# The last stage of an eight-layer kernel: a routing table summed on TensorE and tokens gathered by it, blocks of two sizes, and half of the shared expert moved behind them

## The chip, the cores and the metric

The kernel runs on one core of a Trainium2 chip. The metric is the time of one execution on the device, in microseconds (us), as the median of the runs shown. Everything computed is float32.

## The reference, cut to what matters

Eight layers follow one another on a residual `x` of 8 x 512 tokens of 256 numbers. Each adds `layernorm(layer(layernorm(x)))`. The first seven are not touched. The last one is a mixture of eight experts with a shared expert:

```python
xf = x.reshape(-1, 256)                       # 4096 tokens
scores = softmax(xf @ w_router)               # 8 experts
expert_weights, expert_indices = top_k(scores, 2)
cw = zeros((4096, 8)).at[arange(4096)[:, None], expert_indices].add(expert_weights)
h = silu(einsum('td,edh->teh', xf, w1)) * einsum('td,edh->teh', xf, w3)   # 512 wide
moe_out = einsum('te,ted->td', cw, einsum('teh,ehd->ted', h, w2))
shared = silu(xf @ ws1) * (xf @ ws3) @ ws2
out = shared / 3 + moe_out * (2 / 3)
```

Each token needs only its two experts, so there are 2 x 4096 = 8192 rows of expert work. Which rows go to which expert is known on the chip only.

## The kernel before

The kernel is written in a tile language: pools hand out buffers, a scheduler lays the instructions of each engine in one fixed order, and semaphores join the engines. SP issues most of the transfers, POOL the indirect ones. A buffer is written again only when its last reader is done, and an instruction that waits holds up all that stands behind it on its engine. The seventh layer (`l3_attn`, lines up to 1690) ends at about 4619 us of the profiled span. All that follows is `l3_ffn`.

**Routing.** `route(b)` runs for each of 8 batches of 512 tokens. It normalizes (L1788), transposes on TensorE (L146), copies to `xT` on ScalarE (L148), multiplies by the router (L1796, `pl`), takes Exp on ScalarE (L1803) and the two best experts on VectorE (L1810, L1811), and leaves one-hot tables `O[0]`, `O[1]` (L1820). The normalized rows stay in SBUF in `xnr`, 260 numbers wide: 256 of data, the token's number, two of its weights and its first expert. `places()` then sums the one-hots (L1829, L1834) and derives on VectorE the position of each token's row among rows sorted by expert (L1843 to L1873), where each expert's rows are filled up to a multiple of `BK` = 256, and the expert `ei` of each block (L1886).

**Sorting through DRAM.** 64 indirect transfers (L1963), one for each 128 tokens and each of their two experts, write the rows of `xnr` to their places in `xs`. `xs` was first filled with a neutral row by one transfer of 10 MB on ScalarE's queue (L1730), and each of the 64 waits for that.

**The shared expert.** `shared(b)` runs for all 8 batches before the blocks. `experts` multiplies by two matrices of 256 x 512 (L1755, `gs`), applies Silu on ScalarE (L1760) and the product on VectorE (L1761). `down` multiplies by the third matrix (L1769). The result, times 1/3 (L1894), is stored to `acc` in DRAM (L1896) and loaded again as `yl` (L1979).

**The blocks.** There are 39 blocks of 256 rows: `NBLK = (8192 + 8 * 255) // 256`, whatever the routing is. `block(j)` reads its expert's number into a register of SP (L1906), loads the three weight matrices of 512 KB each (L1740) into a pool with two buffers for each, and loads 256 rows of `xs` (L1912). Nine small instructions on POOL (L1918 to L1931) compute the weight and the destination of each row. TensorE transposes (L1935, `pxb`), VectorE copies (L1938, `xbT`), `experts` and `down` follow with 256 rows as the moving operand, ScalarE applies the weight (L1943), and two indirect transfers on POOL (L1944) write the rows to `ys`, two rows for each token.

**The end.** For each batch two loads of `ys` (L1992) wait for every one of the indirect writes, and VectorE adds them to `yl` (L1997). `add_norm` follows: statistics on VectorE, here with Ln and Exp on ScalarE (L111, L112) for the inverse root because `K.log_exp` is set, the scaling on ScalarE (L172), the addition to `x` on POOL (L174), and the store of the output (L2019).

PSUM is cut into two banks for `pmm` (transposes and routing), four for `pG` (the first two products) and two for `pY` (the third).

Of the kernel before, what the change touches and what calls it, by code (L numbers as in the profile page):

```python
# [1692 lines left out]
def l3_ffn(K):  # L1693
# [4 lines left out]

    nc, tc = K.nc, K.tc
# [5 lines left out]
    BK = 256  # L1705
    NBLK = (2 * NB * L + E * (BK - 1)) // BK
    with ExitStack() as es:
        def pool(name, bufs, **kw):
            return es.enter_context(tc.tile_pool(name="f3" + name, bufs=bufs, **kw))
        dr = pool("dr", 1, space=DRAM)  # L1710

        R_ID, R_DW, R_W1, R_E0, R_END = D, D + 1, D + 2, D + 3, D + 4
        xs = dr.tile([NBLK * BK, R_END], F32, name="xs")
        acc = dr.tile([NB * L, D], F32, name="acc")
        ys = dr.tile([2 * NB * L + 1 + NBLK * BK, D], F32, name="ys")
        cst, wp, sb, s1, s3 = pool("c", 1), pool("w", 2), pool("a", 2), pool("b", 1), pool("d", 3)
        sx = pool("x", 5)
# [4 lines left out]
        zero = cst.tile([P, R_END], F32, name="zero")  # L1722
        nc.vector.memset(zero, 0.0)
        zi = cst.tile([P, 1], I32, name="zi")
        nc.gpsimd.iota(zi, [[1, 1]], base=2 * NB * L + 1, channel_multiplier=1)
        nc.vector.tensor_copy(zero[:, R_ID:R_ID + 1], zi)
        half = cst.tile([P, 2], F32, name="half")
        nc.vector.memset(half, 0.0)
        nc.vector.memset(half[:, 1:2], float(P))
        cleared = nc.scalar.dma_start(  # L1730
            out=xs.rearrange("(n p) d -> p n d", p=P),
            in_=zero[:, None, :].to_broadcast([P, NBLK * BK // P, R_END]))
        ti = cst.tile([P, TT], I32, name="ti")
        nc.gpsimd.iota(ti, [[2 * P, TT]], base=1, channel_multiplier=2)

        def load_weights(src, uid, sel):
            ts = []
            for nm, s, k in zip(("w1", "w3", "w2"), src, (2, 2, 4)):
                t = wp.tile([P, k, s.shape[-1]], F32, tag=nm, name=f"{nm}_{uid}")
                nc.sync.dma_start(out=t, in_=sel(s).rearrange("(k p) n -> p k n", p=P))  # L1740
                ts.append(t)
            return ts

        def experts(xT, n, ws, uid):
# [3 lines left out]
            hT = (s1 if n == L else sb).tile([P, 4, n], F32, tag=f"hT{n}", name=f"hT{uid}")  # L1748
# [15 lines left out]
        def down(hT, ts, w2, uid):  # L1764

            ps = pY.tile([P, 2, D], F32, tag="y", name=f"y{uid}")
            for j, n in enumerate(ts):
                for c in range(4):
                    nc.tensor.matmul(  # L1769
                        ps[:, j, :], lhsT=hT[:, c, n * P:(n + 1) * P], rhs=w2[:, c, :],  # L1770
                        start=(c == 0), stop=(c == 3))
            return ps

        def shared_weights(uid):
            return load_weights([i["l3f_s1"], i["l3f_s3"], i["l3f_s2"]], uid, lambda s: s)


        XN, O = [], []
        for j in range(2):
            O.append(cst.tile([P, E, TT], F32, name=f"O{j}"))  # L1780

        def route(b):
            xn = cst.tile([P, NT, R_END], F32, name=f"xnr{b}")
            XN.append(xn)
            x = K.X[b]
            mv, r = K.stats([x[:, n, :] for n in range(NT)], "ln")
            for n in range(NT):
                nc.vector.tensor_scalar(  # L1788
                    xn[:, n, 0:D], x[:, n, :], mv[:, n, 0:1], r[:, n:n + 1], ALU.subtract, ALU.mult)

            dst = spare[:, b - 5] if b >= 5 else None
            t = K.norm_T(b, sx, pmm, "mm", xn=xn, dst=dst)
# [21 lines left out]
            nc.vector.tensor_scalar(v8, v8, 2.0 / 3.0, None, ALU.mult)  # L1814
            nc.gpsimd.tensor_copy(xn[:, :, R_ID], ti[:, b * NT:(b + 1) * NT])
            nc.vector.tensor_tensor(xn[:, :, R_DW], v8[:, :, 0], v8[:, :, 1], ALU.subtract)
            nc.gpsimd.tensor_copy(xn[:, :, R_W1], v8[:, :, 1])
            nc.gpsimd.tensor_copy(xn[:, :, R_E0], f8[:, :, 0])
            for j in range(2):
                nc.vector.tensor_tensor(  # L1820
# [3 lines left out]
            return t  # L1824

        def places():

            M = cst.tile([P, E, TT], F32, name="M")
            nc.vector.tensor_tensor(M, O[0], O[1], ALU.add)  # L1829
            ones = cst.tile([P, P], F32, name="ones")  # L1830
            nc.vector.memset(ones, 1.0)
            ps = pmm.tile([P, 2, E, TT], F32, tag="mm", name="prank")
            for j, t in enumerate((K.up, ones)):
# [4 lines left out]
            keep = cst.tile([P, E, TT], F32, name="keep")  # L1838
            nc.vector.memset(keep, 1.0)
            nc.vector.memset(keep[:, :, 0:1], 0.0)  # L1840
            cnt = cst.tile([P, E, TT], F32, name="cnt")
# [5 lines left out]
            nb = cst.tile([P, E], F32, name="nb")  # L1847
            nbi = cst.tile([P, E], I32, name="nbi")
            nc.vector.tensor_scalar(nb, cnt[:, :, TT - 1], BK - 1.0, None, ALU.add)
            nc.vector.tensor_copy(nbi, nb)  # L1850
            nc.vector.tensor_single_scalar(
                nbi, nbi, BK.bit_length() - 1, ALU.arith_shift_right)
            nc.vector.tensor_copy(nb, nbi)
            end = cst.tile([P, E], F32, name="end")
            nc.vector.tensor_tensor_scan(end, ones[:, 0:E], nb, 0.0, ALU.mult, ALU.add)
            base = cst.tile([P, E], F32, name="base")
            nc.vector.tensor_tensor(base, end, nb, ALU.subtract)

            pos = cst.tile([P, E, TT], F32, name="pos")
# [3 lines left out]
            nc.vector.scalar_tensor_tensor(  # L1863
                pos, base[:, :, None].to_broadcast([P, E, TT]), float(BK), pos,
                ALU.mult, ALU.add)
            rows = []
            for j in range(2):
                t = cst.tile([P, E, TT], F32, name=f"pj{j}")
                nc.vector.tensor_tensor(t, O[j], pos, ALU.mult)
                f = cst.tile([P, TT], F32, name=f"pf{j}")  # L1870
                nc.vector.tensor_reduce(f, t.rearrange("p e n -> p n e"), AX.X, ALU.add)
                r = cst.tile([P, TT], U32, name=f"row{j}")
                nc.vector.tensor_copy(r, f)  # L1873
                rows.append(r)
            jt = cst.tile([P, NBLK], I32, name="jt")
            nc.gpsimd.iota(jt, [[1, NBLK]], base=0, channel_multiplier=0)
            jf = cst.tile([P, NBLK], F32, name="jf")
            nc.gpsimd.tensor_copy(jf, jt)
            ge = cst.tile([P, NBLK, E - 1], F32, name="ge")
            nc.vector.tensor_tensor(  # L1880
                ge, jf[:, :, None].to_broadcast([P, NBLK, E - 1]),
                end[:, None, 0:E - 1].to_broadcast([P, NBLK, E - 1]), ALU.is_ge)
            ef = cst.tile([P, NBLK], F32, name="ef")
            nc.vector.tensor_reduce(ef, ge, AX.X, ALU.add)
            ei = cst.tile([1, NBLK], I32, name="ei")
            nc.vector.tensor_copy(ei, ef[0:1, :])  # L1886
            return rows, ef, ei
# [95 lines left out]
        for j in range(NBLK):  # L1983
            block(j)
# [115 lines left out]
```

## Time and profile before

| What | us |
|---|---|
| median of 3 runs (5361.62 to 5367.62) | 5366.64 |
| profiled execution, its own time | 5409.07 |
| its span | 5407.4 |
| end of the seventh layer | 4619 |
| routing, places, sorting, shared expert | 4619 to 4894 |
| 39 blocks | 4894 to 5337 |
| the end | 5337 to 5407 |

The profile is of one execution. Its engines are PE (TensorE's matmuls), PEld (its weight loads), DVE (VectorE), ACT (ScalarE), POOL (GpSimd) and SP (the queue of transfers). The times of rows are counted from the start of the span. A float32 matmul shows as two instructions, a transpose as one. The chain of waits follows the last instruction back to what released it, step by step; the timeline gives instructions in order of time; a table of stretches gives the busy time of each engine in a stretch, the number of instructions behind it, the granted clock of TensorE, the busy share of the 16 DMA engines and the GB/s that they moved.

### The profile page before, as it was taken

How to read it: one execution, taken by the hardware profiler on the slowest of the kernel's cores; microseconds unless marked ns; L12 is line 12 of the kernel's file. 1: busy time of each engine (PE TensorE's matmuls, PEld its weight loads, DVE VectorE, ACT ScalarE, POOL GpSimd, SP SyncE). 2: the span in 40 equal slices, each digit the busy share in tenths (PEclk: the TensorE clock that was granted, in tenths of full speed). 3: DMA queues.
4: the chain of work that ended last, by engine and by line, in shares of the span. 5: the costliest groups of instructions: out<-in, count | busy, mean ns of one | idle time of the engine just before them, and what ended most of it. 6: DMA issues, size and time to landing. Idle time of an engine off the chain costs nothing.

```text
span 5407.4 us, 56107 instructions
## 1 busy us (share of the span) xinstructions
PE 4455.9 (82%) x18522; PEld 2698.1 (50%) x18522; DVE 3009.1 (56%) x8102; ACT 1895.8 (35%) x3800; POOL 1941.1 (36%) x1571
## 2 busy tenths in 40 slices
PE   8655888999974987888888899788888887679994
PEld 3334765655554974444444455333333333447883
DVE  7999555477684125455555443387777778411114
ACT  5401324343431332333333324355555554211112
POOL 0001213443432441111111100198878889322332
PEclk9777889999997998999999999898999998889997
DMA  4386511000005970000000000011111111425664
GB/s 120 85 202 152 140 33 41 5 9 5 9 23 133 251 195 8 5 5 4 5 5 1 1 20 1 16 53 44 44 44 45 46 43 51 135 76 170 187 186 157
DMA packets 418856, 371.95 MB, mean 69 GB/s; under 512 B 209827, under 2 KB 354933, under 8 KB 418005
## 3 DMA queue, kind: packets, MB, share of 16 engines
q1 hardware_dynamic: 380564, 309.40, 20.8%
q0 software_dynamic: 16320, 31.78, 2.1%
q10 hardware_dynamic: 21680, 27.18, 1.5%
q8 instruction: 147, 2.41, 0.2%
q14 instruction: 145, 1.18, 0.1%
HBM read 282.13 MB, written 85.91 MB: 68 GB/s over the span
## 4 chain that ended last, share of the span: by engine, by line
PE 39%; DVE 15%; POOL 5%; ACT 5%; issue 4%; another core or an unknown queue 1%; DMA 1%; DVEq 0%; POOLq 0%; SPq 0%; ACTq 0%
DVE h L1667 6%; PE gb L1755 5%; PE T L1402 4%; PE h L1234 3%; PE S L1379 3%; PE y L1638 3%; PE g L1495 3%; PE yb L1769 3%; DVE junk L1384 2%; PE py L185 2%; DVE dB L1613 2%; PE pc L1560 2%; PE gs L1755 2%; PE y L1245 2%; POOL h L1670 2%
## 5 line engine op out<-in xcount | busy, mean ns | idle before, releaser
L1670 POOL TENSOR_TENSOR h<-h,C 128x1024 f32<-128x1024 f32 x256 | 595.8, 2355 | 177.2 <-DVE h L1667 139.3
L1638 PE MATMUL y<-h,C 128*128 128x512 f32 x1024 | 533.9, 662 | 103.0 <-POOL h L1670 103.0
L1667 DVE TENSOR_TENSOR_SCAN h<-dA,dB 128x512 f32<-128x512 f32 x512 | 589.3, 1204 | 29.8 <-ACT dA L1664 12.2
L1664 ACT ACTIVATE dA<-dl,A 128x512 f32<-128x512 f32 x512 | 352.6, 691 | 412.2 <-DVE h L1667 411.1
L929 POOL TENSOR_SCALAR p<-p,rs 128x128 f32<-128x128 f32 (+3 forms) x256 | 275.7, 1086 | 384.6 <-DVE rs L928 222.0
L1638 PEld LDWEIGHTS y<-h,C 128*128 128x128 f32 x1024 | 202.1, 208 | 411.9 <-issue 224.6
L1379 PE MATMUL S<-KT,qz 128*128 128x512 f32 (+3 forms) x1024 | 345.3, 473 | 42.8 <-ACT qz L1367 21.3
L174 POOL TENSOR_TENSOR X<-X,yn 128x1024 f32<-128x1024 f32 x64 | 152.6, 2384 | 613.6 <-ACT yn L172 552.6
L1405 ACT ACTIVATE PT<-T 128x256 f32<-128x256 f32 (+3 forms) x512 | 211.6, 437 | 386.6 <-PE T L1402 378.8
L1402 PE MATMUL T<-qz,KT 128*128 128x512 f32 (+3 forms) x1024 | 313.9, 450 | 2.9 <-DVE mx L1384 0.3
L1407 POOL TENSOR_SCALAR_AFFINE_SELECT PT<-PT 128x512 f32<-128x512 f32 x128 | 81.2, 635 | 632.0 <-ACT PT L1405 628.7
L1618 POOL TENSOR_TENSOR dB<-du,B 128x2048 f32<-128x2048 f32 x64 | 289.8, 4528 | 0.1
L1379 PEld LDWEIGHTS S<-KT,qz 128*128 128x128 f32 x1024 | 181.3, 195 | 209.6 <-DVE mx L1384 60.0
L1755 PE MATMUL gb<-xbT,w_b 128*128 128x256 f32 x1248 | 277.2, 380 | 8.3 <-ACT yb L1943 7.9
L1384 DVE CUSTOM_DVE_ANT_0 junk<-S,mask 128x256 f32<-128x256 f32 (+3 forms) x512 | 250.8, 490 | 58.2 <-PE S L1379 12.1
L1755 PEld LDWEIGHTS gb<-xbT,w_b 128*128 128x128 f32 x1248 | 235.5, 190 | 43.7 <-ACT yb L1943 11.9
L1613 DVE TENSOR_TENSOR dB<-du,pb 128x2048 f32<-128x2048 f32 x64 | 145.5, 2275 | 168.3 <-PE pb L1610 118.7
L1402 PEld LDWEIGHTS T<-qz,KT 128*128 128x128 f32 x1024 | 170.8, 192 | 133.9 <-issue 86.1
L1761 DVE TENSOR_TENSOR hTb<-sb,gb 128x512 f32<-128x512 f32 x78 | 53.7, 688 | 297.5 <-PE gb L1755 297.5
L927 ACT ACTIVATE p<-p,nm 128x128 f32<-128x128 f32 (+3 forms) x256 | 143.8, 563 | 197.3 <-DVE nm L923 192.4
L1239 ACT ACTIVATE hT<-h,w_l_ffn 128x128 f32<-128x128 f32 x384 | 109.5, 368 | 219.1 <-PE h L1234 219.1
L1234 PE MATMUL h<-xgT,w 128*128 128x128 f32 x1536 | 183.6, 278 | 0.0
(492 smaller groups left out, 9086.3 us busy)
## 6 DMA issues: line engine op xcount, KB each, us to landing
w_b<-l3f_w SPq DMA_DIRECT2D x117, 512.0 KB
w<-l1f_w SPq DMA_DIRECT2D x48, 1024.0 KB
C<-xdd SPq DMA_DIRECT2D x128, 256.0 KB
B<-xdd SPq DMA_DIRECT2D x64, 256.0 KB
w<-l1f_w SPq DMA_DIRECT2D x48, 256.0 KB
toep<-l0fd SPq DMA_DIRECT2D x32, 320.0 KB
xs<-zero ACTq DMA_DIRECT2D x1, 10140.0 KB
xb<-xs SPq DMA_DIRECT2D x39, 260.0 KB
```

Source lines behind the costliest of these rows:

```text
L929: nc.gpsimd.tensor_scalar(p[:, 0:n], p[:, 0:n], rs, None, ALU.mult)
L1234: nc.tensor.matmul(ph[:, j, :], lhsT=w1[:, s, c, m * P:(m + 1) * P], rhs=xgT[:, c, :], start=(c == 0), stop=(c == 1))
L1379: nc.tensor.matmul(ps[:, 0:n], lhsT=QZ[:, j, qt * P:n], rhs=KT[:, g, 0:n], start=True, stop=True)
L1384: nc.vector.tensor_tensor_reduce(out=junk[:, 0:n], in0=tiles[j][:, 0:n], in1=mask[:, L - n:L], scale=1.0, scalar=-3.0e38, op0=ALU.add, op1 ...
L1402: nc.tensor.matmul(ps[:, 0:n], lhsT=KT[:, g, kt * P:(kt + 1) * P], rhs=QZ[:, j, kt * P:L], start=True, stop=True)
L1613: nc.vector.tensor_tensor(dB, du, pb[:, None, :].to_broadcast([P, 4, L]), ALU.mult)
L1618: nc.gpsimd.tensor_tensor(dB, du, B[:, None, :].to_broadcast([P, 4, L]), ALU.mult)
L1638: nc.tensor.matmul(py[2 * j + c], lhsT=K.ident, rhs=h[:, c, :], start=False, stop=(n == NS - 1))
L1664: nc.scalar.activation(dA, dl[:, c, :], AF.Exp, scale=A[:, c, n:n + 1])
L1667: nc.vector.tensor_tensor_scan(hs[-1][:, c % 2, :], dA, dB[:, c, :], 0.0, ALU.mult, ALU.add)
L1670: nc.gpsimd.tensor_tensor(h, h, C[:, None, :].to_broadcast([P, 2, L]), ALU.mult)
L1755: nc.tensor.matmul(ps[:, q, :], lhsT=ww[:, k, (c + q) * P:(c + q + 1) * P], rhs=xT[:, k, :], start=(k == 0), stop=(k == 1))
```

## The change

Before the blocks:

- `route` keeps the normalized rows in tiles of a two-buffer pool and stores them to `xn_d` in DRAM in token order, one transfer of 512 KB for each batch. The transposed rows stay in `TS[b]`. The fields beside the rows are gone; the two weights are kept in `WT`.
- `places` fills 256-row blocks first: each expert gets as many full blocks of 256 as its count holds, up to 25 (`NBIG`) in all; the rest goes into blocks of 128, of which there are 21 (`NSMALL`). This adds some 20 small VectorE instructions.
- `table` is new. Each row has a place `128 * hi + lo`. For groups of eight columns VectorE builds a matrix `A` with a one at `lo`, a matrix `B` with a one at `hi`, and `V`, which is `B` times the token's number and times its weight. TensorE sums `A^T V` over all 64 columns into one PSUM bank. What comes out is, for each of 71 half blocks of 128 places, the token, its weight, and where its result goes.
- The 10 MB clearing transfer and the 64 indirect writes are gone.
- The shared expert runs for the first four batches here and leaves its result in SBUF, in `TS[b]`; the store to `acc` and the load back are gone.

In the blocks: a block of 256 is followed by one of 128 as long as there are any, four blocks of 256 come last. Each half block's rows are gathered by an indirect transfer on POOL from `xn_d`, into a pool of six buffers. The nine small POOL instructions are gone. The weight pool has three buffers for each matrix.

Behind the blocks: the shared expert of the last four batches, among the final additions. The loads of `ys` use the weight pool's nine buffers. `K.log_exp` is not set, so `add_norm` takes the inverse root on VectorE (13 small instructions, L90 to L118 of the helper).

```diff
-    BK = 256
-    NBLK = (2 * NB * L + E * (BK - 1)) // BK
+    ROWS, BK = 2 * NB * L, 2 * P
+    NBIG = -(-(ROWS - E * (BK - 1)) // BK)
+    NSMALL = (ROWS - NBIG * BK + E * (P - 1)) // P
+    NBLK, NH = NBIG + NSMALL, 2 * NBIG + NSMALL
+    BEFORE = NB // 2
...
-        cleared = nc.scalar.dma_start(
-            out=xs.rearrange("(n p) d -> p n d", p=P),
-            in_=zero[:, None, :].to_broadcast([P, NBLK * BK // P, R_END]))
...
+            xn = K.norm(b, sb)
+            nc.sync.dma_start(
+                out=xn_d[b * L:(b + 1) * L].rearrange("(n p) d -> p n d", p=P), in_=xn)
+            t = K.norm_T(b, sb, pmm, "mm", xn=xn, dst=TS[b])
...
+        def table(cst, sb, hi, lo):
...
+            ps = pmm.tile([P, 2, NH], F32, tag="mm", name="ptable")
+            S = 8
+            for j in range(2):
+                for c in range(0, TT, S):
+                    A = sb.tile([P, S, P], F32, tag="oa", name=f"oa{j}_{c}")
+                    nc.vector.tensor_tensor(
+                        A, at[:, None, :].to_broadcast([P, S, P]),
+                        lo[:, j, c:c + S, None].to_broadcast([P, S, P]), ALU.is_equal)
+                    B = sb.tile([P, S, NH], F32, tag="ob", name=f"ob{j}_{c}")
+                    nc.vector.tensor_tensor(
+                        B, at[:, None, 0:NH].to_broadcast([P, S, NH]),
+                        hi[:, j, c:c + S, None].to_broadcast([P, S, NH]), ALU.is_equal)
+                    V = sb.tile([P, S, 2, NH], F32, tag="ov", name=f"ov{j}_{c}")
+                    nc.vector.tensor_tensor(
+                        V, B[:, :, None, :].to_broadcast([P, S, 2, NH]),
+                        val[:, j, c:c + S, :, None].to_broadcast([P, S, 2, NH]), ALU.mult)
+                    for n in range(S):
+                        nc.tensor.matmul(
+                            ps.rearrange("p v h -> p (v h)"), lhsT=A[:, n, :],
+                            rhs=V[:, n].rearrange("p v h -> p (v h)"),
+                            start=(j == 0 and c + n == 0), stop=(j == 1 and c + n == TT - 1))
...
-            xb = s3.tile([P, 2, R_END], F32, tag="xb", name=f"xb{j}")
-            ld = nc.sync.dma_start(
-                out=xb, in_=xs[j * BK:(j + 1) * BK].rearrange("(n p) d -> p n d", p=P))
...
+            for n, h in enumerate(his):
+                xb = sb.tile([P, D], F32, tag="xb", name=f"xb{j}_{n}")
+                nc.gpsimd.indirect_dma_start(
+                    out=xb, out_offset=None, in_=xn_d[:, :],
+                    in_offset=bass.IndirectOffsetOnAxis(ap=tok[:, h:h + 1], axis=0))
...
+            for b in range(NB):
+                route(b, sb)
+            table(fc, sb, *places(fc))
+            Y = [shared(b, ws) for b in range(BEFORE)]
...
+        for j in range(NBIG):
+            block(j, (2 * j, 2 * j + 1), sb)
+            if j < NSMALL:
+                block(NBIG + j, (2 * NBIG + j,), sb)
...
-        K.log_exp_tables()
-        K.log_exp = True
         for b in range(NB):
-            y = Y[b]
-
+            y = Y[b] if b < BEFORE else shared(b, ws)
             for t in range(2):
-                c = XN[2 * (b % 4) + t][:, :, 0:D]
+                c = wp.tile([P, NT, D], F32, tag=("w1", "w3", "w2")[(2 * b + t) % 3], name=f"c{b}_{t}")
...
```

## The prediction

> **What bounds the kernel now.** I read the page's slices first, then a table of stretches of the last stage, then the chain of waits there, then the timeline of what the chain names. Of the stretches, the blocks, the end, the front, and 80 us within the front:
>
> ```profile
> 4894.00:5337.00 443.00, 434.75 (x2020) 367.98 (x2019) 77.91 (x116) 78.65 (x155) 142.17 (x399) 1.00 0.59 180
> 5337.00:5407.40 70.40, 0.00 (x0) 0.00 (x0) 48.64 (x112) 21.63 (x51) 22.64 (x10) 0.52 0.55 183
> 4619.00:4894.00 275.00, 203.72 (x717) 125.92 (x718) 68.03 (x363) 50.22 (x81) 71.10 (x120) 0.83 0.33 109
> ...
> 4690.00:4770.00 80.00, 27.20 (x69) 13.87 (x68) 2.07 (x3) 3.49 (x6) 60.22 (x63) 0.64 0.40 140
> ```
>
> The columns after the length are PE, PEld, DVE, ACT and POOL busy, the granted clock, DMA share and GB/s. The blocks are bound by PE (435 of 443 us, full clock). The end has no PE work at all. In 80 us of the front PE, DVE and ACT hardly work while POOL issues the 64 indirect writes. The chain of waits says the same:
>
> ```profile
> 4695.75 50.28 another core or an unknown queue
> 4746.03 11.22 DVEq L1761
> 4757.99 18.83 another core or an unknown queue
> 4777.66 3.78 PE gs L1755 x4
> ...
> 4789.37 13.73 PE gs L1755 x32
> 4803.11 6.91 PE ys L1769 x32
> ...
> 4900.99 3.71 PE yb L1769 x16
> 4904.69 6.91 PE gb L1755 x32
> ...
> 5332.97 3.72 PE yb L1769 x16
> 5339.26 2.39 DMA ys<-yb,it
> ```
>
> One batch of the shared expert is 13.73 + 6.91 = 20.6 us of PE. One block is 443/39 = 11.36 us: 6.91 + 3.72 of matmuls, the rest transposes and short waits. The timeline gives two more: the pace of matmuls with 128 moving columns (fourth layer), and where the places are begun now.
>
> ```profile
> 1762.17 3.65 PEld L1234 LDWEIGHTS h<-xgT,w 128*128 128x128 f32 x32
> ...
> 4680.41 0.42 DVE L1829 TENSOR_TENSOR M<-O,O 128x256 f32<-128x256 f32 x1
> ...
> 5383.36 2.29 DVE L113 SCALAR_TENSOR_TENSOR onh<-onmv,ony 128x4 f32<-128x4 f32 x1
> ```
>
> **The change part by part.**
>
> *Front, routing.* The same matmuls, Exps and reductions. The instruction order of the changed kernel puts the norm of the first two batches before the last statistics of the seventh layer, so their 8 x 0.41 us and the first transposes start some 7 us earlier. The norm of batch b + 2 now waits for the store of batch b, with DVE's queue behind it; the indirect write of the chain took 2.39 us from issue to landing, and a batch takes 6 us of routing, so I count nothing; if each of six waits cost 2.4 us it would be 14. The shared weights are issued behind two stores and after the seventh layer's last matmul, because they go into its slot: 1.5 MB at the 335 GB/s of the clearing transfer is 4.7 us, beside the first norms. The places begin at 4680 now; I take 4677, and 4670 to 4690 as ends.
>
> *Places.* M to the rows took 7.3 us (4680.4 to 4687.7). About 20 more small instructions at 0.16 to 0.2 us, four more of 256 elements at 0.42 us, and three products of the shared expert that stand between them (0.69 us each) make it 15 us.
>
> *Table.* DVE: 8 x (A 1024, V 1136, B 568 elements). The addition of 128x1024 (L1997) takes 1.2 us, so A 1.2, V 1.33, B 0.75: 8 x 3.28 = 26.3 us. Where POOL works beside DVE such an addition took 2.2 us, which would be 52; POOL has nothing to do there, so I take 26. PE: 64 matmuls of 142 columns are 128 instructions; 128 columns go at 3.65/32 = 0.114 us, 256 at 0.216, so 0.12: 15.4 us, paced by DVE.
>
> *Where the blocks begin.* The order on PE leaves behind DVE's last table product: two groups of table matmuls (3.8), the rest of batch 1 (4.3), most of batch 2 (0.9 + 6.9 + 6.9) and batch 3 (20.6), 43 us. So M + 15 + 26.3 + 43 = 4677 + 85 = 4762. In these 43 us POOL issues nine gathers at 0.96 + 0.30 us and SP the weights of three blocks (4.7 MB, 16 us at the 302 GB/s below), then reads 43 expert numbers at 0.57 us (39 do now): all hidden behind PE's shared work. Three queues are passed: ACT's and DVE's work waits on nothing of it. I add 3 us for the burst of gathers: 4765 instead of 4894. Of these 129 us, 4 x 20.6 = 82 are moved, the rest is the stall that goes, less the table.
>
> *The stall, row and rule.* In the 80 us, PE works 27: 53 are lost, and ACT and DVE start again within 8 us of the last indirect write. I read it as something that the long run of indirect writes holds up, perhaps the engines' own instructions. The Trainium skill, "Runtime: NRT & Kernel Launch", section Instruction fetch mechanics, speaks against that reading: refilling instructions is mostly hidden. By the rule the stall has another cause and may stay: then the front gains 53 us less. By the row, 78 indirect writes in pairs among the blocks bring no stall (PE 435 of 443), and the new ones come in threes. I take the row.
>
> *Blocks.* 25 of 256: 25 x 11.36 = 284. A block of 128: 32 instructions of 0.114 (3.65), eight of 256 columns (3.72/2 = 1.86), two transposes (8 take 1.04: 0.26), and 0.25 us for one product of 0.69 us on DVE (L1761) behind only six transposes (0.78): 6.0; 21 x 6.0 = 126. Together 410 instead of 443. The skill's "TensorE: Matmul & The Clock Gate", Back-to-back issue gap, gives 81 ns for 128 columns beside weight loads: 32 x 33 ns less for each block, 22 us in all. The row is float32 of the same shape in this kernel: 114 ns stands. No lost clock is expected; it is 1.00 where PE is dense.
>
> The work that hides the rest: 46 instead of 39 weight loads of 1.57 MB. A pair moves 3.15 + 0.39 gathered + 0.39 written = 3.93 MB in 17.4 us, 226 GB/s. The queue that carries them in the blocks now (packets, MB, share of 16 engines) moved
>
> ```profile
> q1 hardware_dynamic: 11618, 16.09, 53.3%
> ```
>
> in 100 us: 16.09 MB at a share of 53.3% is 302 GB/s at full share, and the fourth layer ran at 250 with PE full:
>
> ```profile
> 1750.00:1800.00 50.00, 50.00 (x415) 46.38 (x414) 7.09 (x16) 18.25 (x64) 20.21 (x16) 1.00 0.96 250
> ```
>
> With three buffers a load has two blocks' time. POOL has six indirect transfers of 1.26 us in a pair, 7.6 of 17.4. The gathers of pair n stand on POOL's queue behind the writes of pair n - 3, so each is issued about two pairs before its transposes.
>
> *End.* T is the last block's end, 4765 + 410 = 5175. PE has 82 us of shared work left. The first addition comes at T + 9 as now (5345.8 after 5336.7). On DVE's queue the fourth product of batch 4 stands behind the additions and norms of four batches: 8 x 1.2, 16 statistics of 0.35 and about 50 small ones, 23 us; so PE can go on at about T + 33, having had 22 to 25 us of work: some 9 us lost, with ends of 0 and 15. So PE ends at T + 92. Behind it: copy 0.7, two additions 2.4, statistics 1.9, 14 dependent small ones 2.8, scaling 2.1, addition on POOL 2.4, store and end 5.3, and waits between them: 18, and 3 for a POOL addition that holds DVE (2.29 us in the row of L113). T + 113 instead of T + 70.
>
> *Sum.* 5175 + 113 = 5288 against the span of 5407: 119 less, say 118. The profiled execution took 5409.07 us, 42 above the median of the runs; I subtract the difference as it is: 5366.64 - 118 = 5249.
>
> **The rivals.**
>
> 1. *The stall stays* in the front or comes back among the blocks, since there are as many indirect transfers as before (142: 64 + 78 and 71 + 71). For: the queue that releases it is not named. Against: the blocks now. 53 us less gain: 5302.
> 2. *The weight loads become the bound.* Bytes: 46 x 1.57 + 142 x 0.131 = 91 MB. If only the 187 GB/s that the blocks show could be had, 487 us instead of 410: gain 41, 5326. Against: the two rates above. At 250 it is 364 us, hidden.
> 3. *PE is faster:* no loss at the end (9), places at 4670 (7), no 0.25 in small blocks (5): 5228.
> 4. *Slower: gathers exposed.* A block that has to wait for its own gathers pays two issues (2.5), a landing (2.39), transposes and copy (1.2): 6 us, 46 times 276, so 5249 + 276 = 5525. It decides against the change from 118/46 = 2.6 us for each block on. For: all gathers stand on POOL behind writes that wait for ACT. Against: the lead of two pairs, 34 us.
>
> **How the numbers follow.** My forecast 0.68, rival 1 0.10, rival 2 0.08, rival 3 0.10, rival 4 0.04. The unknown costs (places 4670 to 4690, loss at the end 0 to 15, burst 0 to 10) are about 20 us either way; down to rival 3 with a little of the 22 us of the rule, up to rival 1: 5215 to 5302. Differences within 0.2% (11 us) count as no change, which is about what a measurement of this kernel tells apart. Faster takes all but rival 4 and 0.02 of rivals 1 and 2 together: 0.94; no change 0.02; slower 0.04.
>
> **What would show it.** Blocks begin near 4765 and take 410 us with PE full; pairs of 17.4 us; no idle of 30 us on ACT or DVE in the front; the table some 26 us of DVE; about 113 us from the last block to the end, with PE idle some 9 us in it. PE idle behind `xb` would be rival 4, behind `w_b` rival 2. A stage that is not shorter by 60 us would make the prediction wrong.

## The result and the profile after

The changed kernel takes 5271.26 us (median of 4 runs, 5262.11 to 5272.13) where the kernel before takes 5367.13 (4 runs, 5361.62 to 5368.12): a ratio of 0.982, 95% interval 0.9803 to 0.9837, or 96 us less. The forecast was 5249 (range 5215 to 5302), 118 less. The sign and the size hold. One term behind them does not, and a second set of errors covered it; the experiments below take that apart.

The profiled execution after has a span of 5269.5 us, and its own time, 5271.25, lies on the median. By stages (front from the last scan product, blocks, end; columns after the length: PE, PEld, DVE, ACT and POOL busy, granted clock, DMA share, GB/s):

```profile
4611.00:4757.00 146.00, 138.59 (x630) 97.27 (x629) 89.74 (x410) 38.53 (x63) 13.49 (x19) 0.95 0.24 78
4757.00:5158.00 401.00, 396.69 (x2175) 347.79 (x2174) 69.88 (x115) 72.51 (x140) 129.93 (x133) 1.00 0.68 213
5158.00:5269.50 111.50, 86.66 (x259) 50.15 (x257) 62.69 (x208) 30.84 (x58) 21.20 (x10) 0.91 0.35 116
```

PE is busy in 138.6 of 146 us of the front, in 396.7 of 401 us of the blocks at full clock, and now works in the end as well. The chain of waits runs over PE from the table into the blocks:

```profile
4711.84 3.97 PE ptable L1929 x32
4715.81 4.32 PE ys L1760 x20
...
4734.76 13.73 PE gs L1746 x32
4748.49 6.91 PE ys L1760 x32
4756.67 7.14 PE gb L1746 x32
4763.81 3.71 PE yb L1760 x16
4767.52 3.58 PE gb L1746 x32
4771.94 1.99 PE yb L1760 x8
4773.94 6.91 PE gb L1746 x32
...
4790.97 6.91 PE gb L1746 x32
```

A big and a small block together take 4773.94 - 4756.67 = 17.27 us at the start and 17.03 behind it (4773.94 to 4790.97). The 128-column matmuls go at 3.58/32 = 0.112 us. The timeline of DVE has the places and the table:

```profile
4676.34 0.43 DVE L1823 TENSOR_TENSOR M<-O,O 128x256 f32<-128x256 f32 x1
...
4689.09 0.74 DVE L1921 TENSOR_TENSOR ob<-at,hi 128x568 f32<-128x568 f32 x1
...
4712.22 1.33 DVE L1925 TENSOR_TENSOR ov<-ob,val 128x1136 f32<-128x1136 f32 x1
4713.47 0.68 DVE L1752 TENSOR_TENSOR hTs<-ss,gs 128x512 f32<-128x512 f32 x1
```

Places take 12.75 us, the table 24.4, and from there to the first block PE has 43.2 us of work. In the end, PE's timeline shows where it waits (in brackets: idle time before the row, and what ended it):

```profile
5158.31 13.90 PE L1746 MATMUL gs<-ts,w_spare_attn 128*128 128x512 f32 x32
...
5173.48 1.99 PE L1760 MATMUL ys<-w_spare_attn,hTs 128*128 128x256 f32 x8 [0.40 <-DVE hTs L1752]
...
5189.27 7.14 PE L1760 MATMUL ys<-w_spare_attn,hTs 128*128 128x256 f32 x20 [4.78 <-DVE hTs L1752]
...
5205.96 5.02 PE L1760 MATMUL ys<-w_spare_attn,hTs 128*128 128x256 f32 x22 [2.23 <-DVE hTs L1752]
...
5245.18 7.07 PE L1760 MATMUL ys<-w_spare_attn,hTs 128*128 128x256 f32 x32
```

PE's last matmul ends 93.8 us after the last block; its work is 4 x 20.65 = 82.6, so 11 us are lost. The waits in these rows are 7.4 of them: 5.2 for products of batch 4, the first batch there, and 2.2 for one of batch 5. Most of the rest is the clock. Behind the longest wait it was granted at 0.50 (the third number from the end) for 5 us:

```profile
5189.27:5194.27 5.00, 5.00 (x12) 3.96 (x13) 4.41 (x18) 2.75 (x7) 2.34 (x1) 0.50 0.46 159
```

The 20 matmuls from 5189.27 take 7.14 us, where 20 at the pace of the last row (7.07/32) take 4.4. Of the wait itself, some 2.1 us are one small instruction of DVE, ahead of the product, that took 2.30 us; its like take 0.12 to 0.17 elsewhere in the end, and POOL had an addition running here:

```profile
5182.07 2.82 POOL L174 TENSOR_TENSOR X<-X,yn 128x1024 f32<-128x1024 f32 x1 [20.55 <-ACT yn L172]
5182.61 2.30 DVE L96 SCALAR_TENSOR_TENSOR ony<-onw,ony 128x4 f32<-128x4 f32 x1
```

**A common zero.** The layers ahead are the same code in both kernels, but they end at other times in each execution: the last product of the scan layer starts at 4600.9 us in the first profile of before, at 4611.0 in that of after, and between 4602 and 4627 in the others below. The granted clock goes with it: from 2000 to 3000 us it is 0.95 in the first profile, 0.94 in that of after, and 0.92 in the three latest (e1, e6, e7). So stages are counted from that product. First before, then after (rows of the line L1670):

```profile
L1670 POOL TENSOR_TENSOR h<-h,C x256: 2332/2353/2400, 3505.3 to 4600.9; 128x1024 f32<-128x1024 f32 x128
```

```profile
L1670 POOL TENSOR_TENSOR h<-h,C x256: 2332/2355/2399, 3514.9 to 4611.0; 128x1024 f32<-128x1024 f32 x128
```

From it to the end the first profile of before took 5407.4 - 4600.9 = 806.5 us, after 5269.5 - 4611.0 = 658.5. That is 148 us less, where the medians differ by 96. About 52 us of the kernel before's profile are not in its timed runs. That gap is the first thing to explain.

### The profile page after: what moved, and what is told of

Same layout as the page of the kernel before. It is cut to its first block, busy times and chain, and to the rows that moved or that the text cites. A ratio compares the mean times of both kernels' runs of the same rounds, so it can differ in the third digit from the quotient of the medians.

```text
span 5269.5 us, 56453 instructions
## 1 busy us (share of the span) xinstructions
PE 4444.4 (84%) x18804; PEld 2705.9 (51%) x18804; DVE 3024.7 (57%) x8229; ACT 1886.4 (36%) x3769; POOL 1866.9 (35%) x1201
## 4 chain that ended last, share of the span: by engine, by line
PE 38%; DVE 16%; ACT 5%; POOL 4%; issue 4%; DMA 1%; POOLq 0%; DVEq 0%; ACTq 0%; SPq 0%
DVE h L1667 7%; PE gb L1746 4%; PE T L1402 4%; PE h L1234 3%; PE S L1379 3%; PE y L1638 3%; PE g L1495 3%; PE yb L1760 2%; DVE junk L1384 2%; DVE dB L1613 2%; PE py L185 2%; PE pc L1560 2%; PE y L1245 2%; PE o L1411 2%; ACT PT L1405 1%
## 5 line engine op out<-in xcount | busy, mean ns | idle before, releaser
L1670 POOL TENSOR_TENSOR h<-h,C 128x1024 f32<-128x1024 f32 x256 | 596.0, 2358 | 177.6 <-DVE h L1667 140.5
L1746 PE MATMUL gb<-xbT,w_b 128*128 128x256 f32 (+1 forms) x1472 | 255.3, 332 | 1.0 <-ACT ts L1950 0.6
```

The costliest lines, as they stand in the source:

```text
L1670: nc.gpsimd.tensor_tensor(h, h, C[:, None, :].to_broadcast([P, 2, L]), ALU.mult)
L1746: nc.tensor.matmul(ps[:, q, :], lhsT=ww[:, k, (c + q) * P:(c + q + 1) * P], rhs=xT[:, k, :], start=(k == 0), stop=(k == 1))
```

## The experiments

**e1: The kernel before, once more** (no edit).

> The kernel before, unchanged, profiled and timed once more. In its first profile the last stage (last product of the scan layer at 4600.9 us to the end at 5407.4) took 806.5 us; the changed kernel's (4611.0 to 5269.5) took 658.5. That is 148 us less, but the medians differ by 96 only. Theory A: the 53 us lost during the 64 indirect writes, forecast to be won, belong to that one profiled execution (5409 us, 42 above the median of the timed runs) and not to an ordinary one. Then a profile whose own time is about 5367 has no ACT idle of 33 us in the front, and about 240 us instead of 293 from the last scan product to the first block. Theory B: the stall is in every execution, the last stage did gain 148, and 52 us were lost in the layers ahead: then a profile of about 5367 shows the stall again and its last stage takes 806 us, the layers ahead some 42 less than 4601. If the new profile is itself at about 5409 with the stall, the two are not told apart by its total and its stages must be set against the timed runs.

Measured: 5363.52 us (20 runs, 5350.64 to 5372.78), ratio to the runs of before beside it 0.9993. Its profile's own time is 5369.85. In the burst (second row) PE works 80 of 80 us, where the first profile had 27:

```profile
4618.00:4855.00 237.00, 207.72 (x756) 131.48 (x757) 73.12 (x379) 52.46 (x87) 75.85 (x123) 0.92 0.39 126
4705.00:4785.00 80.00, 80.00 (x251) 47.50 (x250) 10.81 (x16) 11.94 (x20) 60.52 (x63) 1.00 0.39 137
```

The indirect writes are as many and as dense (63 in the 80 us, POOL busy 60.2 and 60.5 us); the stall is not there. The scan product comes at 4618.1, and the blocks are

```profile
L1755 PE MATMUL gb<-xbT,w_b x1248: 379/379/455, 4855.0 to 5293.7; 128*128 128x256 f32 x179
```

Scan product to first block: 236.9 us instead of 292.9. The total from the scan product is 750.0. Theory A holds: an execution that takes the time of the timed runs does not have the stall. The two profiles add up: the front is 56.0 us shorter here and the layers ahead 17.2 longer, which makes the 39 us between their own times. The instruction queues differ too. DMA queues in 70 us of the burst, first profile of before (packets, MB, share of 16 engines):

```profile
q0 software_dynamic: 2670, 7.45, 29.6%
q1 hardware_dynamic: 1056, 1.05, 4.9%
```

and in this one:

```profile
q0 software_dynamic: 2736, 7.59, 30.0%
q1 hardware_dynamic: 1829, 2.04, 9.4%
q8 instruction: 2, 0.03, 0.2%
q14 instruction: 3, 0.02, 0.2%
```

With the stall, no packet of instructions moved in 70 us; without it five did. That fits engines that wait for their next instructions, but it may also follow from the stall: engines that stand still need none. And one thing speaks against it. In the first profile the engines went on by single steps, 11.1 to 11.2 us apart, without any packet of instructions after 4700:

```profile
4734.85 0.60 ACT L1894 ACTIVATE acc<-ys 128x512 f32<-128x512 f32 x1 [33.12 <-remote]
4746.06 0.60 ACT L1760 ACTIVATE ss<-gs 128x512 f32<-128x512 f32 x1 [10.61 <-remote]
...
4757.30 0.69 DVE L1761 TENSOR_TENSOR hTs<-ss,gs 128x512 f32<-128x512 f32 x1 [61.55 <-issue]
...
4768.44 0.60 ACT L1760 ACTIVATE ss<-gs 128x512 f32<-128x512 f32 x1 [21.79 <-remote]
```

Four matmuls on PE followed each of the last three. What released the engines, these rows do not name ("remote" is another core or an unknown queue, "issue" nothing that the profile shows). The cause of the stall stays open.

**e2: All eight batches of the shared expert in front.**

```diff
-    BEFORE = NB // 2
+    BEFORE = NB
```

> The changed kernel with all eight batches of the shared expert ahead of the blocks. Theory: the half behind the blocks hides the additions and norms of the end. Putting it back makes the blocks begin 4 x 20.6 = 82 us later (4839 if the profile's layers ahead are as before) and the end after the last block 70 us instead of 111: 41 us slower than 5271, so 5312. Rival: the move is worth nothing by itself, since PE has the same work either way and the four batches in front were free cover for the table: 5271. Second rival: the end without log and exp tables and with the loads in weight buffers is longer than 70 us: up to 5325.

Measured: 5317.6 us (ratio to before 0.9908, 0.9889 to 0.9926), 46 more than the changed kernel. The rows of gb give the stage (first and last matmul start):

```profile
L1746 PE MATMUL gb<-xbT,w_b x1472: 272/379/455, 4837.4 to 5235.1; 128*128 128x256 f32 x100, 128*128 128x128 f32 x84
```

The scan product was at 4608.3: 229.1 us to the first block (145.7 in the changed kernel), 401.8 of blocks (401.8), 74.6 of end (111.0). Total 705.5 against 658.5, so the move is worth 47.0 us. It was expected at 41; the end is 74.6 instead of 70.

**e3: Blocks of 256 only.**

```diff
-    NBIG = -(-(ROWS - E * (BK - 1)) // BK)
-    NSMALL = (ROWS - NBIG * BK + E * (P - 1)) // P
+    NBIG, NSMALL = ROWS // BK + E - 1, 0
...
-            big = shifted("big", n_e, 8)
+            nup = tile("nup", E)
+            nc.vector.tensor_scalar(nup, n_e, BK - 1.0, None, ALU.add)
+            big = shifted("big", nup, 8)
...
-            for j, (at, n) in enumerate(((0, NBIG), (NBIG, NSMALL))):
+            for j, (at, n) in enumerate(((0, NBIG),)):
```

> The changed kernel with blocks of 256 alone (39 of them, none of 128); gathers, table and shared half stay. Theory: the two sizes bring 443 - 402 = 41 us, the blocks cost 11.36 us each as before: 5271 + 41 + 2 for a table of 78 instead of 71 columns = 5314. Rival: part of the shorter block stage comes from the gathered form (no read of an expert number per row on POOL, fewer waits): a pair of 256 and 128 takes 17.03 us and the last blocks of 256 10.6 to 12.0; at 11.1 us a block 433, so 5304 or less. The opposite: two gathers for each block in a row with nothing small between make PE wait for them: over 5320.

Measured: 5312.06 us (ratio 0.9891, 0.9871 to 0.991), 41 more than the changed kernel.

```profile
L1745 PE MATMUL gb<-xbT,w_b x1248: 379/379/454, 4754.7 to 5193.4; 128*128 128x256 f32 x179
```

The blocks take 442.8 us, the same as the 442.8 of the kernel before in e1: gathered tokens make a block of 256 neither faster nor slower. By stages the two sizes bring 41.0 us in the blocks, 2.5 in the front, 3.2 in the end, 46.7 together (41 in the medians).

**e4: The end in another order.**

```diff
-        for b in range(NB):
+        for b in (4, 0, 1, 5, 2, 3, 6, 7):
```

> The changed kernel with the last batches in the order 4, 0, 1, 5, 2, 3, 6, 7 instead of 0 to 7, so that DVE takes the products of batch 4 ahead of the additions and norms of batches 0 to 3. Theory: the 11 us of idle PE between the last block (5158.3) and the last matmul (5252.1) go, and the end is 11 us earlier: 5260, PE's 82.6 us of work ends T + 84. Rival: the norms that are pushed back hold up the products of batches 5 to 7, PE waits there instead, and it stays at 5271.

Measured: 5271.91 us: no difference from the changed kernel's 5271.26. PE ends 95.2 us after the last block (93.8 before the edit). The waits moved, they did not go:

```profile
5173.20 7.57 PE L1760 MATMUL ys<-w_spare_attn,hTs 128*128 128x256 f32 x26 [2.86 <-DVE hTs L1752]
...
5222.46 7.33 PE L1760 MATMUL ys<-w_spare_attn,hTs 128*128 128x256 f32 x26 [2.90 <-DVE hTs L1752]
```

**e5: All shared products ahead of the additions.**

```diff
+        Y += [shared(b, ws) for b in range(BEFORE, NB)]
         for b in range(NB):
-            y = Y[b] if b < BEFORE else shared(b, ws)
+            y = Y[b]
```

> The changed kernel with the four batches of the shared expert behind the blocks given out ahead of all additions and norms of the end, so that their products come before these on DVE. In the reordering of e4 the idle time of PE did not go: it moved from batch 4 (4.8 and 2.2 us) to batches 4, 5 and 6 (2.9, 1.4, 1.2, 2.9), since each norm still stood ahead of a later batch's products. Theory: with all products first PE's 82.6 us run in T + 84 to T + 86 and the end is T + 102 to T + 104 instead of T + 111: 5263. Rival: additions and norms (5.7 us of DVE for each batch) pile up behind PE's end: T + 111 or later, 5271 or more.

Measured: 5267.74 us (5 runs, 5264.72 to 5271.13). By its stages it is no gain: PE ends 94.8 us after the last block, the end is 112.0, the total from the scan product 660.5 against 658.5. But the theory is not tested: the edit did not bring the products ahead of the additions on DVE. All eight additions of batches 0 to 3 still run there (5162.30 to 5180.9) before the first product of batch 5 (5183.65). PE waits behind that second batch now:

```profile
5198.78 8.69 PE L1760 MATMUL ys<-w_spare_attn,hTs 128*128 128x256 f32 x26 [5.12 <-DVE hTs L1752]
```

The surprise of these runs is the kernel before. They were made on another chip, and it took 5423.48 us there (9 runs, 5404.64 to 5436.71), so that e5's ratio is 0.9711 (0.9692 to 0.973), 156 us. The changed kernel's variants on that chip took 5268 to 5280.

**e6: Five norms ahead.**

```diff
-            xn = K.norm(b, sb)
+            xn = K.norm(b, fn)
...
+            fn = pool("n", 5, front)
```

> The changed kernel with five tiles for the normed rows of the front instead of two, so that the scheduler lets five norms run ahead of the first batch's routing on DVE (before: all eight). From the last scan product to M (sum of the one-hot rows) the changed kernel takes 65.3 us, the kernel before 79.5; there PE waited 12 us for the first batch's Exp and copy, which stood behind the norms on DVE. Theory: the two tiles made the front shorter, by holding norms back: with five, three more norms of 2 us stand ahead, M comes at 69 to 73 us and the time is 5275 to 5279. Rival: the 14 us come from something else (the 10 MB that is no longer cleared, the rows no longer filled on POOL), and M stays at 65: 5271.

Measured: 5276.72 us, which is just what the theory said, and still it falls. M comes 67.0 us after the scan product; in the kernels without this edit it comes at 65.2 to 66.7, once at 69.2 (e8). The end of this profile is late because its layers ahead were: the scan product came at 4623.4. Norms held back are not what made the front shorter.

The profiles show what did. In the kernel before (e1) the first norm stands behind the clearing of a tile on DVE, which waits for the scan layer's last addition, 18.4 us after the scan product:

```profile
4636.33 0.28 DVE L1723 MEMSET zero<- 128x260 f32 x1 [4.56 <-POOL X L174]
4636.53 0.41 DVE L1788 TENSOR_SCALAR xnr<-X,lnmv,lny 128x256 f32<-128x256 f32 x1
```

In the changed kernel the first two norms run 5.1 us after it:

```profile
4616.10 2.69 DVE L133 TENSOR_SCALAR xn<-X,lnmv,lny 128x256 f32<-128x256 f32 x8
```

The norms start 13.3 us earlier, and M comes 14.2 us earlier (65.3 instead of 79.5). e6 starts them at the same 5.1 us, and keeps its M. The start alone does not decide: in e8 the norms begin 6.8 us before the scan product, ahead of sums of the seventh layer (L1628), and M comes later, at 69.2. No run put the clearing back alone, so this is read from the profiles and not shown by an edit.

**e7: A shorter lead of the gathers.**

```diff
-                xb = sb.tile([P, D], F32, tag="xb", name=f"xb{j}_{n}")
+                xb = sb.tile([P, D], F32, tag="xb", bufs=3, name=f"xb{j}_{n}")
```

> The changed kernel with three tiles for gathered tokens instead of six: the gathers lead by one pair of blocks instead of two. Theory: a pair of 17.0 us is still longer than three issues of 1.26 us and a landing of 2.4 to 2.8, so nothing is exposed: pairs of 17.0 us, 5271 (at most 5 more at the start). Rival (the slower case of the prediction): gathers now stand close enough behind the writes on POOL that PE waits for them, 6 us once in a pair: 21 x 6 = 126, 5397, with PE idle behind xb.

**e8: Two buffers for the weights.**

```diff
-        cst, wp = pool("c", 1), pool("w", 3)
+        cst, wp = pool("c", 1), pool("w", 2)
```

> The changed kernel with two buffers for the experts' weights instead of three. Theory: the loads have room: a pair needs 3.15 MB in 17 us, and a load of 1.57 MB (5.2 us at 302 GB/s) still has the 9 us from one block's last gate matmul to the block after next: pairs stay at 17.0 us, 5271 (at most 10 more). Rival (the second of the prediction): the loads were only just hidden, and with two buffers PE waits for w_b behind each small block, 2 us or more of 46: 5363 or more.

Measured: 5280.21 us (5267.04 to 5289.97) and 5275.57 (5269.78 to 5282.2). The stage that each would lengthen, e7 first:

```profile
L1746 PE MATMUL gb<-xbT,w_b x1472: 272/379/454, 4773.5 to 5172.5; 128*128 128x256 f32 x100, 128*128 128x128 f32 x84
```

```profile
L1746 PE MATMUL gb<-xbT,w_b x1472: 272/379/454, 4762.4 to 5160.1; 128*128 128x256 f32 x100, 128*128 128x128 f32 x84
```

The blocks take 403.1 us with the shorter lead and 401.8 with two buffers (401.8 in the changed kernel): 1.3 us and nothing. Both of the prediction's costly rivals are far off. For the blocks, half the lead and two thirds of the buffers would do; outside of them e8's profile is 5.6 us longer, 3.8 of it in the front, where M comes late.

**e9 and e11: The burst with pauses**, in the kernel before.

```diff
+        now = cst.tile([P, 2, NT], U32, name="now")
         for b in range(NB):
+            for _ in range(12):
+                for j in range(2):
+                    nc.gpsimd.tensor_copy(now[:, j], rows[j][:, b * NT:(b + 1) * NT])
...
-                        out_offset=bass.IndirectOffsetOnAxis(ap=rows[j][:, col:col + 1], axis=0),
+                        out_offset=bass.IndirectOffsetOnAxis(ap=now[:, j, n:n + 1], axis=0),
```

> The kernel before with pauses in its burst: the 64 indirect writes in eight groups of eight, and ahead of each group 24 copies of 4 elements on POOL that rebuild the group's list of rows, so that each group waits for the last writes of the one before (2.4 us) and some 4 us of copies. The 64 writes then take some 125 us instead of 80, which batches 1 to 7 of the shared expert still cover (in e1's profile the writes end at 4786 and the blocks begin at 4855). On one chip the kernel before took 5364 us with PE busy all through the burst, on another 5423, as in the first profile with its stall. Theory A (a long unbroken run of indirect writes keeps the engines from getting their next instructions, on some chips): where the kernel before takes about 5420, the pauses let the fetches through and this takes 5360 to 5375; where it takes about 5364, this is the same. Theory B (the cause is the number of indirect writes, or not in the burst at all): it takes as long as the kernel before on either chip.

> The same kernel as e9 once more, since e9 ran on a chip where the kernel before takes 5363 us and nothing is there to be won. There it took 5382: its writes end 27 us later (at 4813), the first gather of sorted rows stands behind them on SP's queue, the store of a shared batch behind that, and PE waits 27 us for ACT. So theory A (on some chips a long unbroken run of indirect writes keeps the engines from their next instructions) now expects about 5380 to 5390 on a chip where the kernel before takes 5420, that is 35 to 45 less; theory B (number of writes, or a cause outside the burst) expects 5420 + 19 = 5440 there. Where the kernel before takes 5363 again it is 5382 again, and the question stays open.

Measured: 5382.03 us beside 5363.37 for the kernel before (1.0038, 1.0025 to 1.0051), then 5381.06 beside 5362.55 (1.0035, 1.0027 to 1.0043). Both times it ran on chips where the kernel before takes its 5363 us, so the two theories are not told apart. The copies also did not stay in front of their groups: the scheduler set many of them between the writes, so that the pauses were shorter than meant.

These 19 us show something else. The waits of e9 from 4795 to 4824 us:

```profile
ACT acc L1894 <- DMA acc<-acc: 40.3, 1, 40.3
...
PE gs L1755 <- ACT ss L1760: 27.1, 1, 27.1
```

and SP's queue there:

```profile
4814.80 1.39 SPq L1912 DMA_DIRECT2D xb<-xs  x3
4816.29 0.41 SPq L1896 DMA_DIRECT2D acc<-acc  x1
```

The loads of sorted rows wait for the 64 writes, the store of a shared batch stands behind them on SP, ACT waits for its tile, and PE for ACT. In e1 the same chain costs the kernel before 8.3 us; in the changed kernel there is neither the sorted copy nor that store:

```profile
PE gs L1755 <- ACT ss L1760: 8.3, 1, 8.3
```

**e10: Additions on POOL.**

```diff
-                nc.vector.tensor_tensor(y, y, c, ALU.add)
+                (nc.gpsimd if b < BEFORE else nc.vector).tensor_tensor(y, y, c, ALU.add)
```

> The changed kernel with the eight additions of batches 0 to 3 at the end (y + c, 128x1024) on POOL instead of DVE. Neither order (e4) nor priority (e5) took away the 11 to 12 us that PE loses behind the last block; what both kept is the pile of DVE work of four batches, 23 us, that is ready before PE needs a product. Theory: without the additions (8 x 1.2 to 2.3 us) the pile is 10 to 14 us, the product comes in time, PE's work ends at T + 86 and the end at T + 104: 5263. Rival: POOL needs 2.36 us for each (8 x 2.36 = 19 us, and it has the residual additions too), slows DVE's two-operand work beside it, and the statistics wait for POOL instead: 5271 or more.

Measured: 5279.01 us (5 runs, 5278.66 to 5285.49; ratio 0.9844, 0.983 to 0.9858). The rival holds: PE ends 105.3 us after the last block, 11.5 later than in the changed kernel, with one long wait:

```profile
5182.15 8.39 PE L1760 MATMUL ys<-w_spare_attn,hTs 128*128 128x256 f32 x26 [11.38 <-DVE hTs L1752]
```

POOL's row and two of DVE's say why:

```profile
5162.97 16.51 POOL L2017 TENSOR_TENSOR ts<-ts,c 128x1024 f32<-128x1024 f32 x7 [5.25 <-DMA c<-ys]
...
5170.13 2.35 DVE L90 TENSOR_SCALAR ony<-onv 128x4 int32<-128x4 int32 x1
...
5177.23 2.26 DVE L96 SCALAR_TENSOR_TENSOR ony<-onw,ony 128x4 f32<-128x4 f32 x1
```

An addition takes 2.36 us on POOL and 1.2 on DVE. DVE's first statistics wait 5.4 us for POOL, and then, while POOL adds, four small instructions on DVE (5170.13 to 5179.5) take 2.19 to 2.35 us each instead of 0.12 to 0.17. That is some 8 of the 11.38 us; the product stands behind them (5181.42).

**e12: Three batches in front.**

```diff
-    BEFORE = NB // 2
+    BEFORE = 3
```

> The changed kernel with three instead of four batches of the shared expert ahead of the blocks. Neither order (e4), nor priority (e5), nor another engine (e10) took away the 11 to 12 us that PE loses behind the last block, where the additions and norms of the front's batches lie ready in one pile. Theory: the pile is the number of batches in front; with three, 17 instead of 23 us of DVE, PE loses 5 to 8 us instead of 11. In front the first gathers land some 115 us after the last scan product, and PE has shared work until 125 (with four: 145.7), so nothing is exposed there: the end is 3 to 6 us earlier, 5266. Rival: PE loses as much as before (the wait is for the first loads and the first product of the first batch behind the blocks, not for the pile): 5271, or the gathers are exposed after all and it is slower. A difference of less than 8 us can't be told from the times and is read from the stages of the profile.

Measured: 5270.67 us (5 runs, 5262.23 to 5275.23; ratio 0.9821, 0.9803 to 0.9839); total from the scan product 658.4 against 658.5. The blocks begin 126.0 us after the scan product, as expected, and nothing is exposed there. PE ends 113.2 us after the last block with 103.2 us of work: 10.0 lost, where 5 to 8 were expected. The rival holds: the loss does not shrink with the pile of finished batches.

So neither the order of the batches (e4, 12.6 us lost), nor e5's edit (12.2), nor the size of the pile (e12, 10.0) changes the 11 us much, and moving work to POOL (e10, 22.7) doubles it. Each time PE waits for a product on DVE, and each time it is slow behind the longest wait: the 26 matmuls there take 7.57 us in e4, 8.69 in e5 and 8.39 in e10, and 5.7 at full pace. No run took away DVE's small instructions of 2.3 us beside POOL's additions, or put the products ahead on DVE. What sets the size of the loss stays open. No variant beats the changed kernel by more than its runs scatter.

## Why the prediction was right, and which step of it failed

The forecast's sum ran from before's profile: 806.5 us from the scan product to the end, less 119. In the runs that count it is 750.0 (e1), and after 658.5: 91.5 less, beside 96 in the medians. The forecast of 118 is the sum of two errors of opposite sign; that it came so near is in part luck.

*The step that failed: "I subtract the difference as it is".* The first profile's own time, 5409, lay 42 us above the median. The prediction took that as a constant on both sides, and at the same time booked 53 us of a stall in the front as a gain. They were the same microseconds: the stall made that execution long, less some 17 us by which its layers ahead were shorter than in e1. e1 has the same program without the stall, 56.0 us shorter from the scan product to the first block and at the time of the median. With the stall out of the base, the prediction's own stages would have given 750.0 - 687 = 63 us of gain. The sign to look for was on the table: an execution 42 us off its median, and a hole of 53 us in it that no wait explained.

*What covered it: the stages after were 28.6 us shorter than worked out* (687.1 forecast, 658.5 measured, both from the scan product).

- Routing to M: 76.1 forecast, 65.3 measured, 10.8 of the 28.6. The prediction read "some 7 us earlier" in the order of instructions and booked 3; the norms start 13.3 us earlier.
- Places 15, measured 12.75; table on DVE 26.3, measured 24.4 (A 1.22, V 1.33, B 0.74 us: the sizes were right, and neighbours overlap a little).
- PE's work behind the table: 43 forecast, 43.2 measured. The burst of gathers, 3 forecast, cost nothing: six were issued by 4725, 30 us before the first block.
- Blocks: 410 forecast, 401.8 measured. A pair takes 17.03 instead of 17.36, 7 us in 21 pairs; the last four big blocks take about 11.0 each instead of 11.36.
- End: T + 113 forecast, T + 111.0 measured; PE's loss 9 (0 to 15) forecast, 11 measured. The longest wait is at the place that was named, the fourth product of batch 4; but some 2.7 us of the 11 are lost clock, for which the sum of the end had no term, so the waits were somewhat smaller than forecast. Behind PE's end 17.2 us instead of 18 + 3.

*The two rules.* Of the stall, the Trainium skill ("Runtime: NRT & Kernel Launch", Instruction fetch mechanics) has it that refilling instructions is mostly hidden. e1 agrees: 80 of 80 us of PE, with five instruction packets arriving. Whether the first profile goes against it is open: no packet came in 70 us, but what the engines waited for is not named there. The prediction set one trace against the rule; the ordinary execution sides with the rule. Of the pitch, the skill's "TensorE: Matmul & The Clock Gate", Back-to-back issue gap, gives 81 ns; the row gave 114 and the blocks ran at 112. The row was the right choice.

*The rivals.* Gathers exposed (6 us a block): 1.3 us in all blocks even with half the lead. Weights as the bound: nothing even with two buffers. The stall that stays (5302): no profile of the changed kernel or of a variant of it has a stall, and e1's of the kernel before has none. PE faster (5228): its places at 4670 came true in effect, its end without a loss did not.

*Where the 96 us are.* From e1 to after 91.5 us: the shared half behind the blocks is worth 47.0 (e2), the two sizes 46.7 (e3), and since each was measured with the other one in place, what is left for table and gathers instead of the sort is -2 us. The medians give 46, 41 and 9, so this rest is small and its sign is not known. Directly, e1 against e2 (which keeps the two sizes): front 7.8 us less, blocks 41.0 less, end 4.3 more. The sort and its 64 writes were already hidden behind the shared expert, all but 8.3 us; taking them away is worth almost nothing by itself. What it does is to let the blocks begin earlier. In e1 the last of the 64 writes is issued 168 us after the scan product (4786.3), and no block can begin before it; in the changed kernel six gathers are issued by 114 us (4725.0), and e12 begins its blocks at 126. That much is read from the profiles; no run moved the shared expert with the sort in place. As the blocks of e1 begin at 237 us, an estimate from these numbers is that three of the four batches (3 x 20.6 = 62 us) could have moved with the sort as it was, and that only the fourth needs the table.

## What to carry to other kernels

Before a gap in a profile is booked as a gain, set the profile's own time against the median: if it is off by the size of the gap, the gap is likely not in the runs that are timed, and one more profile of the unchanged kernel settles it. Compare two executions from the last instruction that both share, since here the unchanged layers alone moved by 25 us; a total that fits a theory (e6) proves nothing if its stage does not. And PE-bound work that covers nothing where it stands can go where PE would stand idle: 47 us here.

## What the runs showed of the hardware

The kernel before had medians of 5363 to 5367 us on three chips, and 5423 (5405 to 5437) on a fourth; the changed kernel's variants e5 to e8 took 5268 to 5280 on that chip, and e4, e10 and e12 5271 to 5279 on others, so that chip is not slow as such. The difference, 56 to 61 us, has the size of the stall of the first profile, and that execution's 5409 us lie among the fourth chip's times and above all others of that kernel (at most 5381). But no profile of the kernel before was taken on that chip: that the two are one thing is likely, and not shown. What the changed kernel no longer has is a run of 64 indirect writes without a pause; its own gathers come six at first and then three at a time, and in its blocks no such stall is seen (PE 396.7 of 401 us).

Two more things are in the rows of the end. Behind a wait of 4.8 us the clock of TensorE was granted at 0.50 for 5 us, and 20 matmuls took 7.1 us instead of 4.4. And small instructions of DVE took 2.2 to 2.4 us instead of 0.12 to 0.17 while an addition ran on POOL (after and e10).
